# Graph convolution, two layers: a block's own-row transposes and products at the end of the preceding group of sums

## The chip, the cores and the metric

The kernel runs on one core of a Trainium2 chip. A core has TensorE (PE: matmuls and transposes, results in PSUM), VectorE (DVE), ScalarE (ACT), GpSimd (POOL) and SyncE (SP), each with its own queue, worked in order. GpSimd issues the gathers (indirect DMAs), SyncE the plain transfers. The metric is the device time of one execution in microseconds (us); lower is better.

## The reference

A graph has 6,250 nodes with 512 features each and 100,000 edges, sorted by their destination. The layer is two Chebyshev convolutions with a normalization between them, on normalized input, added to the input:

```python
norm = -dinv[src] * dinv[dst]                 # dinv = 1/sqrt(number of edges out of a node)
def prop(h):                                  # sum over the edges into each node
    return segment_sum(h[src] * norm[:, None], dst, num_segments=N)
def _cheb_conv(x, W0, W1, b):
    return x @ W0 + prop(x) @ W1 + b

h = relu(_layernorm(x))
h = _cheb_conv(h, W1_0, W1_1, b1)
h = layer_norm(h, gamma, beta)
h = where(h >= 0, h, 0.01 * h)
out = x + _cheb_conv(h, W2_0, W2_1, b2)
```

All is in float32. For each layer and each node, one row of 512 numbers has to be fetched per incoming edge and summed, and two products with 512 x 512 matrices have to be formed: that of the node's own row with W0, and that of the summed rows with W1.

## The kernel before

**Edges: chunks, units, groups.** The edges are cut into 782 chunks of 128 per layer. One gather fetches the 128 source rows of a chunk (2 KB each) into a slot of `places`, a ring of slots in SBUF. In layer 0 the first slots come from lent tiles too; from then on the ring has `R` = RE + NB - 2 KD = 14 + 49 - 8 = 55 slots, and it shrinks later. Three chunks make a unit, four units a group: a group has 12 chunks, and there are 66 groups per layer (group 0 has a single unit, so group g begins with chunk 3 x (4g - 3) for g > 0). `gather_to`, at the head of a group, issues all gathers whose slots were last used by groups before it; in GpSimd's queue each waits until the sums that used its slot are done.

**Sums.** For a group, VectorE forms selection matrices (`choose`, L650; in layer 0 also scaled by a column that the gather brought, `scale`, L690). `sums` runs 12 products of 128 x 32 by 128 x 512 (two matmuls each, L706), four units side by side into one PSUM tile `ps`. ScalarE copies it to `agg` (L721; in some early groups of layer 0 the tile is named `pre`).

**Blocks.** The nodes are cut into 49 blocks of 128. A block's summed rows lie in two or three neighbouring groups (`inside[i]`); it is due in the first group after these (`inside[i].stop`), so that three of four groups have one due block. For example block 2 is due in group 6, block 3 in group 7, block 4 in group 8, none in group 9, block 5 in group 10. The steps of a block are:

- `own`: four transposes of the block's own rows (tile `h`, loaded two blocks ahead by SyncE, or rows kept in SBUF) into the PSUM tile `hT_ps` (L596), and a copy by ScalarE to `hT` (L598, one buffer).
- `place`: two or three products of a 0/1 matrix `there` (VectorE, L729) with `agg`, into `an_ps` (L742). ScalarE scales the result to `an` (L841).
- `first_half`: four transposes of `an` into another `hT_ps` tile (L849; the name has two buffers), a copy by VectorE to `aT` (L851), and the products of `hT` with the layer's own-row matrix, eight matmuls (L608), into a new tile `u_ps` (two buffers), kept in `started[i]`.
- `second`: eight more matmuls of `aT` with the other matrix into the same `u_ps` (L608), and then `finish`: bias, normalization and leaky relu on VectorE and ScalarE (L810 to L824) and a store to the table of layer 1, or in layer 1 the result and its store to the output.

**Order.** The queues of TensorE, GpSimd and SyncE are in the order of the program; those of VectorE and ScalarE are put in order by the framework's planner. `turn` does `own`, then `second` of the blocks that wait for it (`left`), then `place` and the scaling, for a block that is due. In a group with a due block, TensorE's order is: `own` of it, `second` of the block before, `place`, the group's sums, `first_half` (transposes of `an`, own-row products). In groups 3 to 5 of layer 0 (`SOON`) the `turn` comes after the sums. From group 54 on (`NS - JOIN`), `second` follows `first_half` directly. The last four blocks (`EARLY`) have their own-row products formed separately. In layer 0 some further matmuls are spread over the groups: those that find the scale of the first 76 chunks (`look_up`, `find`, done by group 5), `end_matrices` after group 13, and from group 33 on the steps of `check`, which tests the assumptions on the edges.

Of the kernel before, what the change touches and what calls it, by code (L numbers as in the profile page):

```python
# [9 lines left out]
F32 = mybir.dt.float32  # L10
# [11 lines left out]
P = 128  # L22
# [13 lines left out]
JOIN = 12  # L36
# [415 lines left out]
def usual_path(tc, have):  # L452
# [8 lines left out]
    SOON = range(3, 6)  # L461
    EARLY = {NB - 4: NS - 13, NB - 3: NS - 11, NB - 2: NS - 9, NB - 1: NS - 7}
# [5 lines left out]
    inside = []  # L468
# [3 lines left out]
    with ExitStack() as es:  # L472
        pool = es.enter_context(tc.tile_pool(name="main", bufs=2))
        psum = es.enter_context(tc.tile_pool(name="main_ps", bufs=2, space=bass.MemoryType.PSUM))
# [3 lines left out]
        own_h, own_x, agg, placed, started, pre, late, theres = {}, {}, {}, {}, {}, {}, {}, {}  # L478
# [112 lines left out]
        def own(layer, i):  # L591

            h, r = own_h.pop(i), rows[i]
            ps = psum.tile([P, KD, P], F32, name="hT_ps")
            for kc in range(KD):
                nc.tensor.transpose(ps[:, kc, :r], h[:r, kc * P : (kc + 1) * P], ident[:r, :r])  # L596
            hT = pool.tile([P, KD, P], F32, name="hT", bufs=1)
            nc.scalar.activation(hT[:, :, :r], ps[:, :, :r], AF.Copy)  # L598
            return hT
# [6 lines left out]
        def products(u_ps, hT, w, r, start, stop, some=range(KD)):  # L606
            for kc in some:
                nc.tensor.matmul(u_ps[:r], hT[:, kc, :r], w[:, kc, :], start=(start and kc == 0),  # L608
                                 stop=(stop and kc == KD - 1))
# [113 lines left out]
        def spots(i, some):  # L723

            r = rows[i]
            there = [pool.tile([P, P], F32, name="there", bufs=3) for _ in some]
            for t, g in zip(there, some):
                m = Q * (unit[g + 1] - unit[g])
                behind[1] = nc.vector.tensor_scalar(t[:m, :r], iota_r[:m, :r], node_of[:m, g : g + 1],  # L729
                                                    -(1.0 + i * P), op0=OP.subtract, op1=OP.is_equal)  # L730
            return there
# [14 lines left out]
        def end_matrices():  # L746

            r = rows[END]
            at = pool.tile([P, D], F32, name="xt")[:, :r]
            nc.vector.tensor_scalar_add(at, iota_r[:, :r], 1.0 + END * P)  # L750
            ps = psum.tile([P, D], F32, name="u_ps")[:, :r]
            nc.tensor.matmul(ps, ones.to_broadcast([P, P]), own_row.pop(0)[:, :r], start=True, stop=True)
            for g, t in end_there.items():
                m = Q * (unit[g + 1] - unit[g])
                nc.vector.scalar_tensor_tensor(t[:m], at[:m], node_of[:m, g : g + 1], ps[:m], op0=OP.is_equal,
                                               op1=OP.mult)
# [72 lines left out]
        def turn(layer, i, left=()):  # L829

            r = rows[i]
            if layer == 1 and i not in EARLY:
                load_x(i)
            if i + AHEAD < NB:
                load(layer, i + AHEAD)
            hT = None if i in EARLY else own(layer, i)
            for k, aT in left:
                second(layer, k, aT)
            place(layer, i, [g for g in inside[i] if i < NB - 1 or g == NS - 1])
            an = pool.tile([P, D], F32, name="an")  # L840
            nc.scalar.activation(an[:r], placed.pop(i)[:r], AF.Copy,  # L841
                                 scale=(ndeg if layer == 1 and i not in EARLY else ndinv)[:r, i : i + 1])
            return hT, an

        def first_half(layer, i, hT, an, between=None):
            r = rows[i]
            ps = psum.tile([P, KD, P], F32, name="hT_ps")
            for kc in range(KD):
                nc.tensor.transpose(ps[:, kc, :r], an[:r, kc * P : (kc + 1) * P], ident[:r, :r])  # L849
            aT = pool.tile([P, KD, P], F32, name="aT", bufs=1)  # L850
            behind[2] = nc.vector.tensor_copy(aT[:, :, :r], ps[:, :, :r])  # L851
            if between is not None:
                between()
            if i not in EARLY:
                started[i] = psum.tile([P, D], F32, name="u_ps")
                products(started[i], hT, w_late[:, 1] if layer else w_sb[1], rows[i], True, False)
            return aT
# [11 lines left out]
        def dense(layer, i, hT, an, between=None):  # L869
            second(layer, i, first_half(layer, i, hT, an, between))  # L870

        def check():

            wrong = pool.tile([1, 8], F32, name="wrong", bufs=1)
            n = 0

            def count(v, op, than):
                nonlocal n
                w = v.shape[-1]
                ok = pool.tile([P, D], F32, name="xt")[0:1, :w]  # L880
                nc.vector.tensor_single_scalar(ok, v, than, op=op)
                nc.vector.tensor_reduce(wrong[:, n : n + 1], ok, AX.X, OP.add)
                n += 1

            for at, num in ((1, min(D, NC - 1)), (1 + D, NC - 1 - D)):
                if num > 0:
                    ps = psum.tile([P, D], F32, name="u_ps")[0:1, :num]
                    nc.tensor.matmul(ps, ident[:, 0:1], dlx[:, at + 1 : at + 1 + num], start=True, stop=False)
                    nc.tensor.matmul(ps, minus, dlx[:, at : at + num], start=False, stop=True)
                    count(ps, OP.is_lt, 0.0)  # L890
                    yield
            of = pool.tile([P, D], F32, name="xt")[0:1, :]
            nc.vector.tensor_sub(of[:, :NU], first[0:1, 1 : NU + 1], first[0:1, :NU])
            count(of[:, :NU], OP.is_gt, float(Q - 1))
            m = NS - 1
            of = pool.tile([P, D], F32, name="xt")[0:1, :]
            nc.vector.scalar_tensor_tensor(of[:, :m], iota_r[0:1, :m], -NQ * UN, first[0:1, unit[1] : NU : NQ],
                                           op0=OP.mult, op1=OP.add)
            nc.vector.tensor_scalar_add(of[:, :m], of[:, :m], -mean[1])
            nc.vector.tensor_mul(of[:, :m], of[:, :m], of[:, :m])  # L900
            count(of[:, :m], OP.is_gt, float(DRIFT * DRIFT))
            count(of[:, m - 1 : m], OP.is_gt, float(drift[m] * drift[m]))
            yield
            halves = [(lo, min(lo + D, NC)) for lo in range(0, NC, D)]
            assert len(halves) == 2
            for j, (lo, hi) in enumerate(halves):
                up = pool.tile([P, D], F32, name="xt")[:, : P - 1]
                nc.vector.tensor_sub(up, ident[:, 1:], ident[:, : P - 1])
                ps = psum.tile([P, D], F32, name="u_ps")[: P - 1, : hi - lo]
                nc.tensor.matmul(ps, up, dlx[:, 1 + lo : 1 + hi], start=True, stop=True)  # L910
                ok = pool.tile([P, D], F32, name="xt")[: P - 1, : hi - lo]
                nc.vector.tensor_single_scalar(ok, ps, 0.0, op=OP.is_lt)
                nc.vector.tensor_reduce(unsorted[: P - 1, j : j + 1], ok, AX.X, OP.add)
                yield
            ps = psum.tile([P, D], F32, name="u_ps")[0:1, 0:1]
            for j in range(2):
                nc.tensor.matmul(ps, unsorted[: P - 1, j : j + 1], ones[: P - 1, 0:1], start=(j == 0), stop=(j == 1))
            nc.vector.tensor_copy(wrong[:, n : n + 1], ps)
            n += 1
            ok = pool.tile([P, D], F32, name="xt")[0:1, 0:1]  # L920
            nc.vector.tensor_reduce(ok, wrong[:, :n], AX.X, OP.add)
            nc.vector.tensor_single_scalar(unseen, ok, 0.0, op=OP.is_gt)
# [9 lines left out]
        for layer in range(2):  # L932
# [4 lines left out]
            i, chosen, left = 0, {}, []  # L937
            for g in range(NS - 1):
# [9 lines left out]
                due = []  # L948
# [68 lines left out]
                    find("hT_ps")  # L1017
                if g < NS - JOIN - 1 and inside[i].stop <= g + 1:
                    theres[i] = spots(i, inside[i])
                for k, (hT, an) in due:  # L1020
                    if g < NS - JOIN:
                        left.append((k, first_half(layer, k, hT, an)))
                    else:
                        dense(layer, k, hT, an)
                if layer == 0:
                    look_up("hT_ps")
                    find("hT_ps")
                    if g >= NS // 2:
                        next(checking, None)
# [378 lines left out]
```

## Time and profile before

| | |
|---|---|
| time, median of three runs | 2024.12 us (2021.15 to 2028.18) |
| the profiled execution, its own time | 2021.31 us |
| span of its profile, first to last instruction | 2019.4 us |
| mean granted TensorE clock | 0.92 of full speed |
| instructions in the profile | 19,064 |
| gathers (L270, L515, L526) | 1,564 |
| moved by DMA | 510.33 MB, 253 GB/s in the mean |

All rows below come from the one profiled execution. A row of the timeline gives the start and the length in microseconds, the engine, the line of the kernel, the operation, the tiles written and read, their shapes and the count of merged instructions; in brackets stands the idle time of the engine ahead of it and what ended it. In rows of groups, the number after the busy time is the mean of one instruction in ns. Matmuls are pipelined, so that the start of the next one tells more than the length printed.

### The profile page before, as it was taken

The numbers are of one execution on the slowest core, as the hardware profiler recorded it, in microseconds if no ns is written. First come the engines' busy times: TensorE is split into PE (matmuls) and PEld (weight loads), VectorE is DVE, ScalarE is ACT, GpSimd is POOL, SyncE is SP. The second block draws the span as 40 slices with busy tenths as digits, with TensorE's granted clock in tenths as the row PEclk, the third lists the DMA queues.
The fourth block names the chain that finished last, engine by engine and source line by source line (L and its number), as shares of the span: only waits on it lengthen the run. The fifth ranks groups of instructions, "written<-read, shape, count | busy, mean of one in ns | idle before, by whom it ended". The sixth has DMA issues, their size and how long they took to land.

```text
span 2019.4 us, 19064 instructions
## 1 busy us (share of the span) xinstructions
PE 1665.2 (82%) x6850; PEld 663.2 (33%) x6850; DVE 681.6 (34%) x1454; ACT 389.0 (19%) x703; POOL 1489.1 (74%) x1578
## 2 busy tenths in 40 slices
PE   5589998677887776888888888888888888888898
PEld 4444443222333222333323322223322323333333
DVE  8975453323244233343352111122111211112221
ACT  7895221111111111111111011011010101011110
POOL 5477777777777777777777777777777777777774
PEclk9889999888998888999999999989999999989999
DMA  9998888887888887888877887787777778788875
GB/s 334 392 376 258 249 252 247 239 241 238 269 248 242 241 243 231 252 258 242 252 237 242 244 255 243 236 247 246 228 243 243 244 234 240 230 253 262 273 234 173
DMA packets 180278, 510.33 MB, mean 253 GB/s; under 512 B 33615, under 2 KB 35389, under 8 KB 180173
## 3 DMA queue, kind: packets, MB, share of 16 engines
q0 software_dynamic: 125120, 415.88, 68.5%
q1 hardware_dynamic: 55013, 93.12, 12.9%
q8 instruction: 56, 0.92, 0.2%
q14 instruction: 49, 0.40, 0.1%
q10 hardware_dynamic: 40, 0.02, 0.0%
HBM read 470.01 MB, written 38.86 MB: 252 GB/s over the span
## 4 chain that ended last, share of the span: by engine, by line
POOL 39%; PE 21%; DMA 17%; issue 16%; DVE 5%; ACT 2%; POOLq 0%; DVEq 0%; SPq 0%; ACTq 0%
POOL places L515 39%; DMA places<-tab,sidx 12%; PE u_ps L608 10%; PE ps L706 6%; PE an_ps L742 3%; DMA places<-tab,lidx 2%; ACT places L576 1%; DVE lo L382 1%; DVE hi L382 1%; PE hT_ps L849 1%; DMA dst_c<-in_dst_dram 1%; DMA places<-in_x_dram,sidx 1%; PE hT_ps L596 1%; DMA tab<-places 1%; DVE st L813 0%
## 5 line engine op out<-in xcount | busy, mean ns | idle before, releaser
L515 POOL DMA_INDIRECT places<-tab,sidx x1191 | 1130.1, 949 | 364.1 <-issue 327.5
L706 PE MATMUL ps<-places,sel 128*32 128x512 f32 x3104 | 511.0, 667 | 143.1 <-DMA places<-tab,sidx 86.6
L742 PE MATMUL an_ps<-agg,there 128*128 128x512 f32 (+1 forms) x554 | 268.6, 617 | 95.8 <-ACT agg L721 91.8
L515 POOL DMA_INDIRECT places<-tab,lidx x270 | 255.5, 946 | 82.3 <-issue 78.9
L706 PEld LDWEIGHTS ps<-places,sel 128*32 128x32 f32 x3104 | 102.0, 117 | 519.2 <-issue 194.6
L650 DVE TENSOR_TENSOR sel<-dlx,nodes_ps 128x384 f32<-128x384 f32 (+3 forms) x134 | 72.3, 541 | 417.5 <-PE ps L706 405.6
L608 PE MATMUL u_ps<-w,hT 128*128 128x512 f32 (+1 forms) x400 | 185.4, 607 | 20.7 <-ACT hT L598 20.2
L721 ACT ACTIVATE agg<-ps 128x512 f32<-128x512 f32 (+2 forms) x130 | 76.2, 588 | 610.0 <-PE ps L706 583.5
L608 PE MATMUL u_ps<-places,hT 128*128 128x512 f32 (+2 forms) x408 | 185.4, 598 | 2.9 <-ACT hT L598 2.9
L742 PEld LDWEIGHTS an_ps<-agg,there 128*128 128x128 f32 (+1 forms) x554 | 104.9, 197 | 216.8 <-issue 108.3
L608 PE MATMUL u_ps<-w,aT 128*128 128x512 f32 x384 | 173.1, 593 | 3.1 <-DVE aT L851 3.1
L608 PE MATMUL u_ps<-places,aT 128*128 128x512 f32 x384 | 173.4, 593 | 0.8 <-DVE aT L851 0.8
L690 DVE TENSOR_TENSOR sel<-sel,places 128x384 f32<-128x384 f32 (+9 forms) x76 | 35.1, 468 | 331.9 <-DMA places<-tab,sidx 331.9
L804 DVE SCALAR_TENSOR_TENSOR u_ps<-u_ps,root,bias 128x512 f32<-128x512 f32 x45 | 34.1, 758 | 284.8 <-PE u_ps L608 284.8
L598 ACT ACTIVATE hT<-hT_ps 128x512 f32<-128x512 f32 (+1 forms) x98 | 58.2, 594 | 291.3 <-PE hT_ps L596 290.9
L608 PEld LDWEIGHTS u_ps<-w,hT 128*128 128x128 f32 (+1 forms) x400 | 73.7, 194 | 96.7 <-issue 74.8
L608 PEld LDWEIGHTS u_ps<-places,hT 128*128 128x128 f32 (+1 forms) x408 | 75.7, 196 | 78.5 <-issue 73.6
L816 ACT ACTIVATE sd<-mv,eps 128x1 f32<-128x1 f32 (+1 forms) x49 | 14.4, 294 | 441.1 <-DVE mv L814 441.1
L270 POOL DMA_INDIRECT places<-in_x_dram,sidx x63 | 59.6, 947 | 52.6 <-ACT junk L286 19.0
L729 DVE TENSOR_SCALAR there<-iota_r,node_of 128x128 f32<-128x128 f32 (+1 forms) x286 | 68.2, 307 | 89.4 <-PE an_ps L742 89.4
L608 PEld LDWEIGHTS u_ps<-w,aT 128*128 128x128 f32 x384 | 70.7, 190 | 83.2 <-issue 78.6
L608 PEld LDWEIGHTS u_ps<-places,aT 128*128 128x128 f32 x384 | 70.6, 190 | 80.3 <-issue 78.3
(200 smaller groups left out, 1245.3 us busy)
## 6 DMA issues: line engine op xcount, KB each, us to landing
places<-tab,sidx POOLq DMA_INDIRECT x1191, 3.8
h<-tab SPq DMA_DIRECT2D x70, 256.0 KB
xt<-in_x_dram SPq DMA_DIRECT2D x48, 256.0 KB
out_dram<-t SPq DMA_DIRECT2D x48, 256.0 KB
tab<-places SPq DMA_DIRECT2D x22, 528.0 KB
places<-in_x_dram SPq DMA_DIRECT2D x5, 1792.0 KB
tab<-t SPq DMA_DIRECT2D x26, 256.0 KB
tab<-places SPq DMA_DIRECT2D x20, 256.0 KB
```

Source lines behind the costliest of these rows:

```text
L270: nc.gpsimd.indirect_dma_start(out=lent[t] if t < X else places[:, t - X, :D], out_offset=None, in_=x, in_offset=bass.IndirectOffsetOnAxis ...
L382: nc.vector.tensor_tensor(t, s[:, g * 2 * GJ : (g + 1) * 2 * GJ].rearrange("p (j s) -> p j s", s=2)[:, :, None, :] .to_broadcast([EP, GJ, ...
L515: nc.gpsimd.indirect_dma_start(out=places[:, slot(t), :] if own_scale else zr(layer, t), out_offset=None, in_=x if layer == 0 and t < RAW ...
L598: nc.scalar.activation(hT[:, :, :r], ps[:, :, :r], AF.Copy)
L608: nc.tensor.matmul(u_ps[:r], hT[:, kc, :r], w[:, kc, :], start=(start and kc == 0), stop=(stop and kc == KD - 1))
L650: nc.vector.tensor_tensor(sel[:, q : q + k, :w, :], of, node[:, q : q + k, None, :].to_broadcast([P, k, w, Q]), op=OP.is_equal)
L690: last = nc.vector.tensor_tensor(v, v, places[:, k : k + hi - lo, D : D + 1].to_broadcast([P, hi - lo, Q]), op=OP.mult)
L706: members.append(nc.tensor.matmul(to, sel[:, q, s, :], rows_of, start=(s == 0), stop=(s == len(chunk[q]) - 1 and (cnt is None or chunk[q][ ...
L721: nc.scalar.activation(agg[g][: n * Q, lo : lo + w], ps[: n * Q, lo : lo + w], AF.Copy)
L729: behind[1] = nc.vector.tensor_scalar(t[:m, :r], iota_r[:m, :r], node_of[:m, g : g + 1], -(1.0 + i * P), op0=OP.subtract, op1=OP.is_equal)
L742: all_of.append(nc.tensor.matmul(placed[i][:r], t[:m, :r], agg[g][:m, :], start=(g == inside[i][0]), stop=(g == inside[i][-1])))
L804: nc.vector.scalar_tensor_tensor(v, v, root[:r, i : i + 1], bias2[:r], op0=OP.mult, op1=OP.add)
```

## The change

At the end of a group, after the sums, the kernel looks at the next block. If it is due in the next group (`inside[i].stop <= g + 1`), fewer than two blocks are due in this one, the group is before group 52 (`NS - JOIN - 2`), and it is layer 1 or group 6 or later, then `own` of that block is issued there, ahead of `first_half` of the block due in this group, and the products of `hT` follow it, into a `u_ps` tile that is kept in `started`. `turn` and `first_half` leave both out for a block that is in `started`. Four helper tiles in PSUM, in `end_matrices` and `check`, take buffers of the name `hT_ps` instead of `u_ps`.

```diff
 def end_matrices():
-            ps = psum.tile([P, D], F32, name="u_ps")[:, :r]
+            ps = psum.tile([P, D], F32, name="hT_ps")[:, :r]
...
 def turn(layer, i, left=()):
-            hT = None if i in EARLY else own(layer, i)
+            hT = None if i in EARLY or i in started else own(layer, i)
...
 def first_half(layer, i, hT, an, between=None):
-            if i not in EARLY:
+            if i not in EARLY and i not in started:
                 started[i] = psum.tile([P, D], F32, name="u_ps")
                 products(started[i], hT, w_late[:, 1] if layer else w_sb[1], rows[i], True, False)
...
 def check():                                   # in three places
-                    ps = psum.tile([P, D], F32, name="u_ps")[0:1, :num]
+                    ps = psum.tile([P, D], F32, name="hT_ps")[0:1, :num]
...
 # the loop over the groups, after the sums of group g
                 if g < NS - JOIN - 1 and inside[i].stop <= g + 1:
                     theres[i] = spots(i, inside[i])
+                ahead_of = (g < NS - JOIN - 2 and inside[i].stop <= g + 1 and len(due) < 2
+                            and (layer == 1 or g >= SOON.stop))
+                if ahead_of:
+                    next_hT = own(layer, i)
                 for k, (hT, an) in due:
                     if g < NS - JOIN:
                         left.append((k, first_half(layer, k, hT, an)))
                     else:
                         dense(layer, k, hT, an)
+                if ahead_of:
+                    started[i] = psum.tile([P, D], F32, name="u_ps")
+                    products(started[i], next_hT, w_late[:, 1] if layer else w_sb[1], rows[i], True, False)
```

More of the change, by code (lines that the diff above doesn't have):

```diff
@@ L908, in check @@
                 nc.vector.tensor_sub(up, ident[:, 1:], ident[:, : P - 1])
-                ps = psum.tile([P, D], F32, name="u_ps")[: P - 1, : hi - lo]
+                ps = psum.tile([P, D], F32, name="hT_ps")[: P - 1, : hi - lo]
                 nc.tensor.matmul(ps, up, dlx[:, 1 + lo : 1 + hi], start=True, stop=True)
@@ L914, in check @@
                 yield
-            ps = psum.tile([P, D], F32, name="u_ps")[0:1, 0:1]
+            ps = psum.tile([P, D], F32, name="hT_ps")[0:1, 0:1]
             for j in range(2):
```

## The prediction

> **What bounds the kernel now.** I read the page first: its span, its busy times, and its chain that ended last.
>
> ```profile
> span 2019.4 us, 19064 instructions
> ## 1 busy us (share of the span) xinstructions
> PE 1665.2 (82%) x6850; PEld 663.2 (33%) x6850; DVE 681.6 (34%) x1454; ACT 389.0 (19%) x703; POOL 1489.1 (74%) x1578
> ...
> POOL 39%; PE 21%; DMA 17%; issue 16%; DVE 5%; ACT 2%; POOLq 0%; DVEq 0%; SPq 0%; ACTq 0%
> ```
>
> TensorE is busier than GpSimd (82% against 74%), yet the chain runs through GpSimd. So the next view is GpSimd's groups of instructions from 129 us to the last gather. Columns: busy time and mean of one, then the idle time just before them and what ended it.
>
> ```profile
> L515 POOL DMA_INDIRECT places<-tab,sidx x1191 | 1130.1, 949 | 364.1 <-issue 327.5 <-DMA places<-tab,sidx 19.8 <-ACT places L576 3.9
> L515 POOL DMA_INDIRECT places<-tab,lidx x270 | 255.5, 946 | 82.3 <-issue 78.9 <-DMA places<-tab,lidx 2.7 <-PE ps L706 0.6
> L526 POOL DMA_INDIRECT places<-tab,eidx x27 | 27.7, 1026 | 8.2 <-issue 7.9 <-DMA tab<-pre 0.3
> ```
>
> The idle time is 364.1 / 1191 = 0.306 us and 82.3 / 270 = 0.305 us per gather, nearly all put down to issue. A gather therefore takes 0.95 us and 0.30 us of pause, 1.25 us, and GpSimd never rests otherwise. These 1,488 gathers at 1.25 us are 1860.0 us; busy and idle times add up to 1867.9. Only 7.9 us in the whole stretch are anything but the bare pace. The timeline of GpSimd gives its ends:
>
> ```profile
> 129.13 0.94 POOL L270 DMA_INDIRECT places<-in_x_dram,sidx  x1 [0.65 <-ACT pre L721]
> ...
> 2000.90 0.94 POOL L515 DMA_INDIRECT places<-tab,lidx  x1 [0.30 <-issue]
> ```
>
> After the last gather, 2019.4 - 2001.8 = 17.6 us are left for its landing, the last sums and the last two blocks. None of that is touched: the change stops at group 51 of 66 in each layer. So the time moves only if GpSimd is made to wait, or is spared a wait. The table by stretches says where that can be. Columns: length of the stretch, busy time of PE, PEld, DVE, ACT and POOL, granted clock, DMA share, GB/s.
>
> ```profile
> 200.00:300.00 100.00, 100.00 (x448) 40.87 (x444) 49.43 (x113) 22.07 (x39) 75.02 (x79) 1.00 0.83 250
> 300.00:650.00 350.00, 272.89 (x1111) 106.81 (x1104) 126.35 (x291) 51.58 (x93) 264.82 (x280) 0.89 0.82 246
> ...
> 1060.00:1500.00 440.00, 373.07 (x1428) 131.60 (x1420) 88.53 (x196) 46.09 (x74) 333.06 (x352) 0.93 0.79 243
> ```
>
> Between 200 and 300 us TensorE is never idle: it has more work ready than it gets done. Later it idles 22% (272.89 of 350) and 15% (373.07 of 440). The place to look at is thus early in layer 0, where TensorE is late and a gather may have to wait for its slot.
>
> **The pinch.** GpSimd's timeline there:
>
> ```profile
> 200.90 1.02 POOL L515 DMA_INDIRECT places<-tab,sidx  x1 [0.30 <-issue]
> 203.33 0.94 POOL L515 DMA_INDIRECT places<-tab,sidx  x1 [1.41 <-ACT pre L721]
> ```
>
> Counted from 0 in GpSimd's order, the gather at 203.33 is number 130. The ring has 14 + 49 - 8 = 55 slots here, so it reuses that of chunk 75, the first of group 7 (3 x 25). It waits for all sums of group 7. TensorE's rows from the end of group 6's sums to the end of group 7's:
>
> ```profile
> 189.23 0.66 PE L849 MATMUL hT_ps<-ident,an 128*128 128x128 f32 x4
> 189.72 3.60 PE L608 MATMUL u_ps<-w,hT 128*128 128x512 f32 x8
> 193.16 0.60 PE L596 MATMUL hT_ps<-ident,h 128*128 128x128 f32 x4
> 193.59 3.60 PE L608 MATMUL u_ps<-w,aT 128*128 128x512 f32 x8
> 197.03 1.02 PE L742 MATMUL an_ps<-agg,there 128*128 128x512 f32 x2
> 197.89 1.02 PE L742 MATMUL an_ps<-pre,there 128*128 128x512 f32 x2
> 198.74 1.02 PE L742 MATMUL an_ps<-agg,there 128*128 128x512 f32 x2
> 199.70 2.78 PE L706 MATMUL ps<-places,sel 128*32 128x512 f32 x24
> 202.41 0.66 PE L849 MATMUL hT_ps<-ident,an 128*128 128x128 f32 x4
> ```
>
> From start to start: transposes of the aggregate 0.49 us, own-row products 3.44, own-row transposes 0.43, second half of a block 3.44, placing 2.67, sums 2.71. The sums of group 7 end at 202.41 and the gather starts 0.92 us later. There is no slack at all: it had already waited 1.41 us instead of 0.30. ScalarE's copies in the same stretch:
>
> ```profile
> 189.33 0.60 ACT L721 ACTIVATE agg<-ps 128x512 f32<-128x512 f32 x1 [0.74 <-PE ps L706]
> 193.85 0.60 ACT L598 ACTIVATE hT<-hT_ps 128x512 f32<-128x512 f32 x1 [3.92 <-PE hT_ps L596]
> ```
>
> A copy of 0.60 us follows the sums by 0.10 us (189.23 to 189.33), and the hT copy follows the end of its transposes by 0.09 us (193.76 to 193.85).
>
> **The change part by part.** Nothing is added or removed. For 35 blocks of layer 0 (3 to 37) and 38 of layer 1 (0 to 37), four transposes, one ScalarE copy and eight matmuls (0.43, 0.60 and 3.44 us) come before the next group instead of within it. No DMA and no GpSimd instruction is among them. SyncE's load of a later h tile waits for the same transposes and comes free no later. Two u_ps tiles are now alive at once, all that there are; the next one needs VectorE to have finished the block before, with placing and sums (2.67 + 2.71 us) between: a wait here would stand where the hT wait stands, and I take 0 for it. Giving u_ps tiles to hT_ps in the end matrices and the checks changes no instruction; what it costs is at most a wait for a buffer in groups with spare TensorE time, taken as 0.
>
> *Group 6, paid once.* Block 2 has not been started early, since the condition begins with this group. So group 6 ends with the products of block 2 and those of block 3: one run of 3.44 us moves ahead of the sums of group 7. In steady state each group loses a run and gains one; here it only gains. There is also a wait: hT has one buffer, so block 3's copy can start only when block 2's products have read it. The aggregate's transposes now start at 189.66, block 2's products at 190.15; they end 3.60 us later, at 193.75. Copy from 193.84 to 194.44, and 0.05 us to TensorE (the row at 806.24 below follows its copy's end at 806.19 by that). TensorE was free at 193.59, so it stands 0.90 us. Together 0.90 + 3.44 = 4.34 us before the sums of group 7, which end at 206.75. Gather 130 starts at 207.67.
>
> *Each later block.* Where a block was also due, TensorE issues own transposes and aggregate transposes (0.43 + 0.49 = 0.92 us), and the products wait for ScalarE's two copies: 0.10 + 0.60 + 0.60 + 0.05 = 1.35 us. New stall: 0.43 us. Where no block was due, the cover is 0.43 us and the stall 0.92. Where no own rows follow, the products no longer cover the aT copy. The trace has that case at the end of layer 1:
>
> ```profile
> 1979.87 3.70 PE L608 MATMUL u_ps<-places,aT 128*128 128x512 f32 x8 [0.78 <-DVE aT L851]
> ```
>
> 0.78 us. In a cycle of four groups (three blocks) that makes 0.92 + 0.43 + 0.43 + 0.78 = 2.56 us on TensorE, in 48 gathers or 60 us. In the later stretches 15% to 22% of 60 us, 9 to 13 us, are idle and hide it; the bounds are 0 and 2.56 us a cycle, and I take 0. If that cover were gone, the 24 such cycles (11 and 13) would cost 61 us.
>
> *The next gather that could wait.* After gather 130 this is number 142, freed by group 8:
>
> ```profile
> 212.88 2.78 PE L706 MATMUL ps<-places,sel 128*32 128x512 f32 x24
> 215.59 0.66 PE L849 MATMUL hT_ps<-ident,an 128*128 128x128 f32 x4
> ```
>
> ```profile
> 218.56 0.95 POOL L515 DMA_INDIRECT places<-tab,sidx  x1 [0.30 <-issue]
> ```
>
> Its sums move by 4.34 + 0.43 = 4.77 us, to end at 220.36, and free it at 221.28. GpSimd, itself 4.34 us late, comes to it at 222.90. It does not wait, with 1.62 us to spare. Group 9 then gives a run of products back (block 4's ran a group earlier), so the lead grows.
>
> *The sum.* GpSimd loses 4.34 us once and keeps its pace after it. The profiled execution took 2021.3 us, 1.9 above its span: 2021.3 + 4.34 = 2025.7 us, 0.21% slower. The median of the runs, 2024.1, lies 2.8 us above that execution; counted from it the same step gives 2028.5. Bounds of the step: 0, if the copies fall so that nothing is late, and 7.4 us with the colder clock below. About 0.3%, 6.1 us, is what a measurement of this kernel can tell from no change, so the forecast counts as no change.
>
> **The clock.** Does a short stall make TensorE slow? After 2.44 us of waiting, the 24 matmuls of a group took 4.32 us instead of the 2.78 above:
>
> ```profile
> 423.46 4.32 PE L706 MATMUL ps<-places,sel 128*32 128x512 f32 x24 [2.44 <-DVE sel L690]
> ```
>
> After 0.78 us, the eight matmuls at 1979.87 took 3.70 instead of 3.60. The new stalls are 0.43 to 0.92 us, so I charge nothing. A rule speaks against this: the Trainium skill (TensorE: Matmul & The Clock Gate, "A second HAM failure mode: psum-queue depth-cycling") says that frequent micro-idles between groups of matmuls can make the clock gate swing to half rate and back. The trace bears it out for 2.44 us, not for 0.78. By that rule the first rival below is the case.
>
> **The rivals.** *Colder clock, a little slower.* Each new stall at the ends of groups 6 and 7 brings one slow start of 4.32 - 2.78 = 1.54 us. The sums of group 7 come 4.34 + 1.54 = 5.88 us late, those of group 8 4.77 + 3.08 = 7.85. Gather 142 is freed at 224.36 and reached at 224.44: it just doesn't wait, and the time is 2021.3 + 5.9 = 2027.2 us; with a third slow start among them, now unspared, 2028.7. For it: the granted clock of 0.89 from 300 us on. Against it: the row after 0.78 us. It decides from stalls of some 1 to 2 us on.
>
> *ScalarE holds hT, slower than before.* In layer 0, ScalarE runs its queue in order, and the statistics of a block (sd) wait for VectorE, which waits for gathers:
>
> ```profile
> 805.41 0.29 ACT L816 ACTIVATE sd<-mv,eps 128x1 f32<-128x1 f32 x1 [30.26 <-DVE mv L814]
> 805.61 0.58 ACT L721 ACTIVATE agg<-ps 128x512 f32<-128x512 f32 x1
> 806.09 0.59 ACT L598 ACTIVATE hT<-hT_ps 128x512 f32<-128x512 f32 x1
> ```
>
> ```profile
> 806.24 2.08 PE L742 MATMUL an_ps<-agg,there 128*128 128x512 f32 x2 [17.66 <-ACT agg L721]
> ```
>
> ```profile
> 812.49 0.95 POOL L515 DMA_INDIRECT places<-tab,sidx  x1 [0.30 <-issue]
> ```
>
> Placing waited 17.66 us for agg; now the products wait as long for hT, and placing comes after them. The hT copy comes 0.48 us after that of agg, and the products take 3.44, so the sums after such a group come 3.9 us later. The gather at 812.49 reuses a slot of group 49, whose copy began at 805.61: 6.9 us of slack. From a delay of more than that, gathers wait, and two such groups past it cost about 2 x 3.9 us: 2025.7 + 7.8 = 2033.5. Against it: one such delay is smaller than the slack, and group 49's own sums lose a run of products.
>
> *No effect.* The planner's order of ScalarE or VectorE offsets the early stall: 2021.3. For it: only 1.1 us of the wait at 203.33 stand against the pace. Against it: TensorE is full there, and 3.44 us are put ahead of what gather 130 needs.
>
> *Faster.* Products would cover TensorE's waits for agg. Against it: GpSimd does not feel those. All that it could regain is 7.9 us, so 2013.4 at the very best, and gaining 6.1 would need three quarters of it.
>
> **How the numbers follow.** Forecast 0.54, colder clock or longer stalls 0.18, ScalarE's queue 0.13, no effect 0.11, faster 0.04. Within 0.3% fall no effect, half of the colder clock (2027.2 is just inside 6.1 us) and 0.42 of the forecast: 0.62. Slower are ScalarE's queue, the other half of the colder clock and the 0.12 of the forecast that I leave to runs scattered upward: 0.34. The likeliest is 2025.7 us. The range reaches from 2020.0 (no effect, in a run like the lowest shown, 2021.2, and 1 us of spread) to 2034.0 (ScalarE's case, or the colder clock's 2028.7 with the 2.8 us of the median and some spread).
>
> **What would show it.** Right: the gather after the twelve that group 6 freed waits about 5 to 6 us (1.41 before), the sums of group 7 end near 206.8, gather 142 does not wait, and the gathers after it keep 1.25 us to the end, with the last one near 2005.2 and the same 17.6 us behind it. New stalls of 0.4 to 0.9 us stand ahead of the own-row products, put down to ACT hT, and 0.8 us ahead of the second half of every third block. Wrong: waits of GpSimd above 0.3 us after 230 us; a wait at gather 130 of 1.41 us or less; another tail after the last gather; or the 24 matmuls of groups 7 to 12 at over 4 us.

## The result and the profile after

The changed kernel takes 2028.1 us in the median of 20 runs (2026.1 to 2032.9), the one before 2024.3 in 20 runs (2021.0 to 2028.2). The ratio is 1.0023, with a 95% interval of 1.0017 to 1.0029: slower by 3.9 us between the medians, within the 0.3% that was set as no change, and clear of zero. The forecast was 4.3 us more than before (2025.7 counted from the profiled execution, 2028.5 from the median).

The profiled execution of the changed kernel lies in the upper part of its runs: 2030.9 us, a span of 2029.1. Its page, busy times and the chain that ended last:

```profile
span 2029.1 us, 19114 instructions
...
PE 1663.1 (82%) x6850; PEld 670.1 (33%) x6850; DVE 687.3 (34%) x1454; ACT 388.6 (19%) x703; POOL 1491.3 (73%) x1578
...
POOL 35%; PE 27%; DMA 15%; issue 14%; DVE 6%; ACT 3%; SPq 0%; POOLq 0%; DVEq 0%; ACTq 0%
```

The counts of TensorE's, VectorE's, ScalarE's and GpSimd's instructions are those of before. GpSimd's groups from 129 us to the last gather (busy time and mean of one, then the idle time before):

```profile
L515 POOL DMA_INDIRECT places<-tab,sidx x1191 | 1131.8, 950 | 372.8 <-issue 326.6 <-DMA places<-tab,sidx 22.2 <-ACT pre L721 9.5
L515 POOL DMA_INDIRECT places<-tab,lidx x270 | 255.6, 947 | 82.3 <-issue 77.1 <-DMA places<-tab,lidx 4.3 <-PE ps L706 0.6
```

The idle time of the first group has grown from 364.1 to 372.8 us, and its third releaser is new: 9.5 us put down to the aggregate's copy of group 7, which starts when that group's sums end. One gather holds nearly all of it. It is number 130, and the last gather follows:

```profile
211.31 0.94 POOL L515 DMA_INDIRECT places<-tab,sidx  x1 [9.23 <-ACT pre L721]
...
2010.81 0.95 POOL L515 DMA_INDIRECT places<-tab,lidx  x1 [0.31 <-issue]
```

Before, that gather started at 203.33 after 1.41 us. The rows of TensorE between the sums of group 6 and those of group 7 tell why:

```profile
192.76 0.66 PE L596 MATMUL hT_ps<-ident,h 128*128 128x128 f32 x4
193.25 0.60 PE L849 MATMUL hT_ps<-ident,an 128*128 128x128 f32 x4
193.69 3.60 PE L608 MATMUL u_ps<-w,hT 128*128 128x512 f32 x8
198.03 3.70 PE L608 MATMUL u_ps<-w,hT 128*128 128x512 f32 x8 [0.75 <-ACT hT L598]
201.57 3.60 PE L608 MATMUL u_ps<-w,aT 128*128 128x512 f32 x8
205.01 1.02 PE L742 MATMUL an_ps<-agg,there 128*128 128x512 f32 x2
205.86 1.02 PE L742 MATMUL an_ps<-pre,there 128*128 128x512 f32 x2
206.72 1.02 PE L742 MATMUL an_ps<-agg,there 128*128 128x512 f32 x2
207.67 2.78 PE L706 MATMUL ps<-places,sel 128*32 128x512 f32 x24
210.39 0.66 PE L596 MATMUL hT_ps<-ident,h 128*128 128x128 f32 x4
```

There are two runs of own-row products now (193.69 and 198.03), with a wait of 0.75 us between by the bracket, or 0.90 us counted from start to start (198.03 - 193.69 - 3.44). The copy that the second run waits for starts 0.09 us after the first run has ended (193.69 + 3.60 = 197.29):

```profile
197.38 0.60 ACT L598 ACTIVATE hT<-hT_ps 128x512 f32<-128x512 f32 x1 [3.92 <-PE u_ps L608]
```

What ended ScalarE's wait is the run of products that reads the one hT buffer. From the end of one group's sums to the end of the next pass 210.39 - 192.76 = 17.63 us; before it was 202.41 - 189.23 = 13.18. That is 4.45 us more, where 4.34 were forecast: the wait is 0.90 us of it, the second run 3.54 (201.57 - 198.03). Gather 130 starts 0.92 us after the sums, as before.

The two profiled spans differ by 9.7 us, though, and not by 4.4. They split up so: 3.53 us because the sums of group 6 ended later (192.76 against 189.23), in a stretch where TensorE's and ScalarE's instructions and their order are the same in both kernels; 4.45 us between groups 6 and 7; 1.93 us between gather 130 and the last one (1799.50 against 1797.57 us), as more of the gathers took over 0.1 us above the pace (22 against 15) and the others a trifle longer, with no new wait; and -0.2 us behind the last gather (17.3 against 17.6). The first part varies from run to run: in six kernels below that are the same up to there (one block alone, without the early groups, the three with repeated products, without the first block), they end anywhere between 190.1 and 195.7 us.

### The profile page after: what moved, and what is told of

Read it like the earlier page. It is cut to its first block, busy times and chain, and to the rows that moved or that the text cites. A ratio compares the mean times of both kernels' runs of the same rounds, so it can differ in the third digit from the quotient of the medians.

```text
span 2029.1 us, 19114 instructions
## 1 busy us (share of the span) xinstructions
PE 1663.1 (82%) x6850; PEld 670.1 (33%) x6850; DVE 687.3 (34%) x1454; ACT 388.6 (19%) x703; POOL 1491.3 (73%) x1578
## 4 chain that ended last, share of the span: by engine, by line
POOL 35%; PE 27%; DMA 15%; issue 14%; DVE 6%; ACT 3%; SPq 0%; POOLq 0%; DVEq 0%; ACTq 0%
POOL places L515 35%; PE u_ps L608 14%; DMA places<-tab,sidx 10%; PE ps L706 6%; PE an_ps L742 4%; DMA places<-tab,lidx 3%; DVE hi L382 1%; ACT hT L598 1%; DVE lo L382 1%; DMA w<-in_L_gnn_W_dram 1%; ACT agg L721 1%; DVE st L813 1%; DVE u_ps L810 1%; DMA places<-in_x_dram,sidx 0%; ACT places L576 0%
## 5 line engine op out<-in xcount | busy, mean ns | idle before, releaser
L515 POOL DMA_INDIRECT places<-tab,sidx x1191 | 1131.8, 950 | 372.8 <-issue 326.6
L706 PE MATMUL ps<-places,sel 128*32 128x512 f32 x3104 | 478.7, 642 | 106.6 <-DMA places<-tab,sidx 68.5
L608 PE MATMUL u_ps<-w,hT 128*128 128x512 f32 (+1 forms) x400 | 209.9, 673 | 140.5 <-ACT hT L598 137.0
L742 PE MATMUL an_ps<-agg,there 128*128 128x512 f32 (+1 forms) x554 | 255.6, 595 | 5.2 <-DVE rs L819 5.2
L608 PEld LDWEIGHTS u_ps<-w,hT 128*128 128x128 f32 (+1 forms) x400 | 81.6, 215 | 238.3 <-ACT hT L598 146.9
L841 ACT ACTIVATE an<-an_ps,ndeg 128x512 f32<-128x512 f32 x45 | 31.0, 688 | 342.0 <-PE an_ps L742 342.0
```

Of the source, the lines that this page charges most:

```text
L515: nc.gpsimd.indirect_dma_start(out=places[:, slot(t), :] if own_scale else zr(layer, t), out_offset=None, in_=x if layer == 0 and t < RAW ...
L706: members.append(nc.tensor.matmul(to, sel[:, q, s, :], rows_of, start=(s == 0), stop=(s == len(chunk[q]) - 1 and (cnt is None or chunk[q][ ...
L742: all_of.append(nc.tensor.matmul(placed[i][:r], t[:m, :r], agg[g][:m, :], start=(g == inside[i][0]), stop=(g == inside[i][-1])))
L841: nc.scalar.activation(an[:r], placed.pop(i)[:r], AF.Copy, scale=(ndeg if layer == 1 and i not in EARLY else ndinv)[:r, i : i + 1])
```

## The experiments

The theory: GpSimd paces the kernel, and the change makes it wait once, at gather 130, for a run of products that now stands ahead of the sums of group 7. The main rival: the 73 moved blocks each add short stalls to TensorE, and these add up. A second one was that TensorE's work is on the path throughout. Ratios are to the kernel before on the same chip, with 95% intervals.

**One block alone.**

```diff
-                            and (layer == 1 or g >= SOON.stop))
+                            and layer == 0 and g == SOON.stop)
```

> The change for one block only: block 3 of layer 0, at the end of group 6. The other 72 blocks stay as before. Theory (GpSimd waits once, at gather 130, for the sums of group 7): the whole cost is here, +4.3 us against before, the ratio 1.002, the same as the full change; gather 130 waits some 4.3 us longer. Rival (the short stalls of the 73 blocks add up): one block of 73, so +0.1 us, ratio 1.000.

Measured: 2029.2 us against 2024.9, ratio 1.0022 (1.0013 to 1.0032). One moved block of 73 costs as much as all. In its trace, TensorE goes from the end of group 6's sums to that of group 7's in 207.75 - 190.12 = 17.63 us, as in the full change:

```profile
190.12 0.66 PE L596 MATMUL hT_ps<-ident,h 128*128 128x128 f32 x4
...
195.40 3.70 PE L608 MATMUL u_ps<-w,hT 128*128 128x512 f32 x8 [0.75 <-ACT hT L598]
...
205.04 2.78 PE L706 MATMUL ps<-places,sel 128*32 128x512 f32 x24
207.75 0.66 PE L849 MATMUL hT_ps<-ident,an 128*128 128x128 f32 x4
```

Its gather 130 waited 4.25 us, which is 2.8 us longer than before and not the 4.3 that were expected, because GpSimd itself came to it later in this execution (204.4 us against 201.9). Set beside the full change, a start 2.6 us earlier (190.12 against 192.76) is most of the difference to 9.23; the rest is where GpSimd stood (it had waited longer earlier).

**All blocks but the early ones.**

```diff
-                            and (layer == 1 or g >= SOON.stop))
+                            and (layer == 1 or g >= 13))
```

> The change without the early groups: layer 0 only from group 13 on, layer 1 as in the change; 30 and 38 of the 73 blocks. Theory of the pinch: gathers of the slots used from group 13 on have over 7 us of slack, so 0 us against before, ratio 1.000 within 0.001, and no wait of GpSimd above 0.3 us after gather 130. Rival of the stalls that add up: 68 of 73 blocks, so +3.6 us, ratio 1.0018.

Measured: 2025.0 us against 2024.9, ratio 1.0004 (0.9993 to 1.0015). 68 blocks cost nothing that can be seen; the 1.0018 of the stalls lies outside the interval. The four helper tiles that take buffers of another name are in this kernel too, so nothing can be seen of them either. GpSimd's groups carry 368.0 us of idle time in the first one (364.1 before), 3.9 us of it at gather 130, where this execution's late start shows (sums of group 6 to 194.06, then 13.19 us, as before).

**The same work twice, without the change, at the pinch and behind it.** In the kernel before, in `first_half`:

```diff
                 started[i] = psum.tile([P, D], F32, name="u_ps")
+                if layer == 0 and i == 2:                 # or: i in range(8, 36, 3)
+                    products(started[i], hT, w_sb[1], rows[i], True, True)
                 products(started[i], hT, w_late[:, 1] if layer else w_sb[1], rows[i], True, False)
```

> The kernel before, with the own-row products of block 2 (layer 0, end of group 6) computed twice: eight matmuls, 3.44 us more on TensorE ahead of the sums of group 7, and nothing moved. Theory of the pinch: +3.4 us against before, ratio 1.0017, though TensorE idles for some 350 us in the whole. Rival (TensorE has room, the cost of the change is in its new waits): 0 us.

Measured: 2028.6 us against 2024.9, but the ratio of 1.0010 has an interval of 0.9999 to 1.0022, which holds the theory's 1.0017 and, just, 1.0000. By the times this is open. The trace shows 212.27 - 195.66 = 16.61 us between the sums, 3.43 more than before, and 8.31 us of wait at gather 130.

> The kernel before, with the own-row products of ten blocks of layer 0 (8, 11, 14 to 35, due in groups 14, 18, 22 to 50) computed twice: 80 matmuls, 34 us more on TensorE, all behind the pinch. Theory: TensorE's idle time in those groups takes them, 0 us against before, ratio 1.000 within 0.001. Rival (TensorE's work is on the path all along): +34 us, ratio 1.017.

Measured: 2024.0 us against 2024.9, ratio 0.9998 (0.9989 to 1.0007). Ten extra runs of products, 34 us of TensorE, cost nothing behind the pinch.

To close what the single extra run left open, the same with four extra runs (`for _ in range(4)` for block 2):

> The kernel before, with the own-row products of block 2 at the end of group 6 computed five times: 32 more matmuls, 13.8 us of TensorE ahead of the sums of group 7, all of it work that the result does not need. Theory of the pinch: nearly all of it arrives at the end, +13 to +14 us, ratio 1.0065, and gather 130 waits about 14 us longer than in the kernel before. Rival (TensorE's later idle time takes it): 0.

Measured: 2038.9 us against 2024.7, ratio 1.0078 (1.0064 to 1.0091), 13 to 18 us. The three rows that carry it, two of TensorE and one of GpSimd:

```profile
191.35 17.33 PE L608 MATMUL u_ps<-w,hT 128*128 128x512 f32 x40
...
215.06 2.78 PE L706 MATMUL ps<-places,sel 128*32 128x512 f32 x24
```

```profile
218.70 0.94 POOL L515 DMA_INDIRECT places<-tab,sidx  x1 [15.20 <-ACT pre L721]
```

The work reaches the end in full: the last gather starts 2015.05 - 218.70 = 1796.4 us after gather 130. In the other kernels of these two sets that have no further wait it is 1796.4 to 1796.9 us, in the one before 1797.6. Behind the last gather pass 17.2 to 17.9 us in all of these. The start of gather 130 thus settles the time, to some 1.5 us.

**Without the first block.**

```diff
-                            and (layer == 1 or g >= SOON.stop))
+                            and (layer == 1 or g >= 7))
```

> The change without its first block: layer 0 from group 7 on, layer 1 as in the change; 72 of 73 blocks. Now the sums of group 8 are the first to get a run of products more ahead of them (4.3 us with the hT wait), and gather 142 has 2.1 us of slack. Theory of the pinch: +2.3 us, ratio 1.0011, the wait at gather 142 and not at 130. Rival of the stalls: as the full change, +4, ratio 1.002.

Measured: 2027.2 us against 2024.7, ratio 1.0017 (1.0008 to 1.0026). Both sizes lie in the interval, so the time doesn't tell the two apart; the place does. The wait appears where the theory puts it, at gather 142:

```profile
225.33 0.94 POOL L515 DMA_INDIRECT places<-tab,sidx  x1 [2.48 <-PE ps L706]
```

It is 2.18 us above the usual 0.30, where 2.3 were expected. This gather follows the end of the sums that it waits for by 0.45 us (224.88 to 225.33), where gather 130 follows ScalarE's copy, 0.92 us after the sums. (Gather 130 waited too, 5.22 us, behind a late start: the sums of group 6 ended at 194.07.) The late start moves both gathers alike, so the slack of some 2 us at the second one stays.

**Relieving the pinch.** If the theory holds, sums that come earlier should gain. Groups 3 to 5 already do their sums first.

```diff
-    SOON = range(3, 6)
+    SOON = range(3, 9)
```

> The kernel before, with groups 6 to 8 of layer 0 also of the kind that does its sums first and the due block after them (as groups 3 to 5 do). The own transposes (0.43), second half (3.44) and placing (2.67) of a block move from ahead of the sums of group 7 to behind them: these come some 6 us earlier. Theory of the pinch: the wait at gather 130 is gone; faster by what it cost, 1 to 5 us as the start of a run falls, ratio 0.998. Rival (the time is set elsewhere): 0.

The same range stands in L717, so that the edit also gives the aggregate of group 9 a tile of the name `pre` instead of `agg`.

Measured: 2026.1 us against 2024.7, ratio 1.0007 (0.9998 to 1.0017). It is not faster: this expectation failed. TensorE's rows show a wait that has grown and a new one:

```profile
176.86 2.78 PE L706 MATMUL ps<-places,sel 128*32 128x512 f32 x24
...
189.75 5.33 PE L706 MATMUL ps<-places,sel 128*32 128x512 f32 x18 [4.62 <-ACT places L576]
195.01 0.86 PE L596 MATMUL hT_ps<-ident,h 128*128 128x128 f32 x4
195.71 1.02 PE L742 MATMUL an_ps<-pre,there 128*128 128x512 f32 x2
196.57 1.02 PE L742 MATMUL an_ps<-agg,there 128*128 128x512 f32 x2
197.43 1.02 PE L742 MATMUL an_ps<-pre,there 128*128 128x512 f32 x2
199.23 0.66 PE L849 MATMUL hT_ps<-ident,an 128*128 128x128 f32 x4 [0.78 <-ACT an L841]
...
203.25 2.78 PE L706 MATMUL ps<-places,sel 128*32 128x512 f32 x24
205.96 0.66 PE L596 MATMUL hT_ps<-ident,h 128*128 128x128 f32 x4
```

The sums of group 6 cannot come earlier, because they need rows that ScalarE still has to scale (L576); they wait 4.62 us instead of 1.84 and run slower after it (5.33 us for 18 matmuls instead of 2.76). What stood ahead of them had been cover. Then the transposes of `an` follow its scaling with nothing between, 0.78 us a block. The sums of group 7 come 2.2 us nearer to those of group 6 (10.95 us against 13.18), but that only makes up for the later sums of group 6: from the start of group 5's sums, up to which TensorE's order is the same in both kernels, to the end of group 7's pass 205.96 - 176.86 = 29.10 us, and before it was 202.41 - 173.41 = 29.00. Nothing was gained ahead of gather 130. It waited 3.77 us in this execution, and gather 154 waited 1.47. This execution also took 2.8 us longer behind the last gather (20.4 us against 17.6), at the end of layer 1, where the edit changes nothing. So the start of the pinch is set by ScalarE as well as by TensorE, which my theory had left out.

> The changed kernel with the same three groups doing their sums first; by its own condition the change then begins at group 9 of layer 0. 33 and 38 blocks keep the change. Theory of the pinch: the cost of the change is gone, the same time as the kernel before with these groups, ratio 0.998 against before. Rival of the stalls: 71 blocks still cost 4 us more than that.

Measured: 2027.6 us against 2024.7, ratio 1.0018 (1.0008 to 1.0028). The expected 0.998 failed here too. The interval overlaps with that of 1.0007, and 1.0018 is also what the rival could give; the difference of the two, 1.5 us, is not clear of noise. In its trace GpSimd has waits at the same two gathers as without the change (1.90 and 1.47 us, there 3.77 and 1.47) and none behind them, which speaks for the theory, but the times settle nothing.

**The wait for the hT buffer, and a second try at relief.** Two more kernels, an own tile for block 3's `hT`, and only groups 7 and 8 with their sums first:

```diff
+            if layer == 0 and i == 3:
+                hT = pool.tile([P, D], F32, name="xt").rearrange("p (k e) -> p k e", k=KD)
+            else:
                 hT = pool.tile([P, KD, P], F32, name="hT", bufs=1)
```

```diff
-                soon = layer == 0 and g in SOON
+                soon = layer == 0 and (g in SOON or g in (7, 8))
```

> The changed kernel with the own rows of block 3 of layer 0 copied to a tile of their own instead of the one hT buffer, so that the copy need not wait for block 2's products. One look at the trace: the wait of TensorE ahead of block 3's products (0.75 us in the changed kernel) is gone, and from the end of the sums of group 6 to the end of those of group 7 pass 16.8 to 16.9 us, against 17.6 in the changed kernel and 13.2 in the one before. The rest of the 4.4 us, the run of products itself (3.4), stays. Rival (the wait is for ScalarE's queue, not for the buffer): 17.6 as before.

> The kernel before, with groups 7 and 8 of layer 0 doing their sums first, and group 6 left as it was (so that its sums do not stand longer for ScalarE's scaling, the 4.6 us seen with groups 6 to 8). The sums of group 7 come right after block 2's products, 6.5 us earlier in TensorE's order. Theory of the pinch: no wait above 0.3 us at gather 130, and what it cost is gained, 1 to 4 us, ratio 0.9985. Rival (as with groups 6 to 8, the new wait of the aggregate's transposes for ScalarE, 0.78 us a block, and the next gathers take it back): 0 or +1 us.

> The same kernel as own3_apart, which fell on a chip where the kernel before takes 2,381 us and GpSimd waits at many places, so that it cannot be set beside the other runs. Expected as there: no wait ahead of block 3's products, 16.8 to 16.9 us from the end of the sums of group 6 to those of group 7 (17.6 in the changed kernel, 13.2 before); in time 0.7 us less than the changed kernel, ratio to before 1.0018, more than these runs can tell. Rival (ScalarE's queue holds the copy): 17.6.

> The same kernel as soon78, for the same reason. Theory of the pinch: no wait above 0.3 us at gather 130, 1 to 4 us gained, ratio 0.9985. Rival (the aggregate's transposes wait 0.78 us a block for ScalarE, and a later gather takes the gain back): ratio 1.000.

All four runs fell on another chip, where the kernel before takes 2381 us and the granted clock is 0.85 to 0.87. GpSimd there waits in many places, mostly 12 gathers after the wait before, and more often than not for what the trace only calls `remote`:

```profile
POOL places L515 <- issue: 396.9, 1290, 4.0
POOL places L515 <- remote: 156.4, 63, 4.3
```

(the waits of GpSimd with the own tile: total, count, longest). On that chip GpSimd is not simply at its pace, so these runs cannot test the pinch. Groups 7 and 8 first gave ratios of 0.9999 (0.9975 to 1.0024) and 0.9988 (0.9968 to 1.0009); both intervals hold 1 as well as the expected 0.9985, so they decide nothing. Gather 130 waited 1.71 us in one of their traces and 0.30 in the other, and gather 142 then 2.60 and 3.36. The changed kernel with the own tile took 18.0 us in both traces from the end of group 6's sums to that of group 7's (245.74 to 263.73 and 240.08 to 258.09), where 16.8 to 16.9 were expected: this expectation failed. Ahead of block 3's products stood a wait of 0.21 us in the single run and of 1.13 in the other, as ScalarE came to its copies late there (its copy of the aggregate began 4.5 us after the sums in both, at 250.24 and 244.60, where it is 0.10 in the kernel before on the ordinary chip). Whether the wait for the buffer can be had back on the ordinary chips stays open. The kernel with the own tile took 2373.4 us against 2381.8 in the second set, ratio 0.9963 (0.9942 to 0.9985), and 2376.4 in the single run. It contains the full change, so there the change, with that tile, gains rather than loses. Which of the two does it, and through what, was not tried.

## Why the prediction was right or wrong, point by point

**What bounds the kernel.** Right, and shown. GpSimd's pace carries the time: 34 us of extra TensorE work behind the pinch cost nothing, 13.8 us ahead of gather 130 cost 13 to 18.

**The step at group 6.** Right in place and size: 4.45 us instead of 4.34. The wait for the one hT buffer is the 0.90 us of the prediction, counted as there from start to start, and the second run of products took 3.54 us instead of 3.44, a slower start that had been charged at nothing. One block alone gives the whole cost. The measured 3.9 us (4.7 by the ratio, whose interval is 3.4 to 5.9) are this step. That gather 130 has no slack is true of the profile from which it was read. In that of the ten repeated products, with the same order up to there, it did not wait: its slot was free at 204.42 + 0.92 = 205.34 us, and GpSimd came to it at 205.76. In such an execution the step would cost 0.4 us less, by this estimate. The single figure of 2025.7 us lies 2.4 below the measured median, as it was counted from a profiled execution 3.0 us below the median of the kernel before; counted from the median, 2028.5, it is met to 0.4.

**The later stalls.** Right that GpSimd does not feel them; from group 13 on they cost nothing. Their sizes, from start to start as the prediction counts: with a block due, 0.47 us instead of 0.43 (0.31 in the brackets); with no block due, 0.9 to 1.0 us instead of 0.92 (0.75 in the brackets, once 1.05) in the early groups, and far longer later, below. With aT uncovered it is the 0.78 us that had been taken from a bracket. No wait is put down to a u_ps buffer, as assumed. TensorE's waits in the changed kernel (total, count, longest):

```profile
PE u_ps L608 <- ACT hT L598: 157.3, 80, 17.6
PE ps L706 <- DMA places<-tab,sidx: 68.5, 43, 6.1
...
PE u_ps L608 <- DVE aT L851: 22.4, 27, 1.6
```

The waits for `agg` ahead of placing, 91.8 us before, are gone from this list, and the waits for gathers fell from 86.6 to 68.5 us. In their place stand 157.3 us ahead of the own-row products (23.2 before). The waits changed their place more than their sum.

**Gather 142.** Right that it does not wait with the full change (0.31 us); without block 3 moved it waited 2.48. Its slot comes free 0.45 us after the sums, not 0.92 as was taken over from gather 130, so that the prediction made the slack 0.5 us too small.

**The colder clock.** This rival did not occur. After waits of 0.31 and 0.75 us the eight matmuls took 3.70 us, and the 24 of groups 7 and 8 still 2.78; the granted clock from 200 to 300 us stayed at 1.00:

```profile
200.00:300.00 100.00, 95.40 (x401) 38.51 (x403) 44.79 (x99) 18.52 (x34) 69.14 (x73) 1.00 0.76 228
```

The Trainium skill's warning about micro-idles (TensorE: Matmul & The Clock Gate, "A second HAM failure mode: psum-queue depth-cycling") is not borne out for pauses of this length. Long ones do show slow starts, as the next row.

**ScalarE holds hT.** The mechanism is there, the cost is not. Where placing had waited 17.66 us, the products now wait as long and then run slowly (5.75 us for eight matmuls instead of 3.60):

```profile
816.00 5.75 PE L608 MATMUL u_ps<-w,hT 128*128 128x512 f32 x8 [17.65 <-ACT hT L598]
```

No gather waited for it: the step from the gather before does not exceed 1.7 us anywhere between there and the end of the layer. The slack of 6.9 us held, as the argument against this rival had it.

**What would show it.** Three numbers came out otherwise: gather 130 waited 9.23 us, not 5 to 6, the sums of group 7 ended at 210.4, not 206.8, and the last gather started at 2010.8, not near 2005.2. The first two are the start of that execution, 3.5 us later, which the prediction took as fixed; the third adds the 1.9 us between gather 130 and the last one. The start is a part of the spread: where gather 130 waits, each microsecond by which the sums of group 6 end later is one by which it starts later, in both kernels.

**No effect, and faster.** Neither occurred. The bound on a gain, 7.9 us of GpSimd time above its pace, was not tested by this change.

## What to carry to other kernels

Where one queue issues without pause, work on the other engines costs nothing until an instruction of that queue has to wait for it, so look for the few places where its waits exceed its pace, and ask of each moved step whether it lands ahead of what they need. A step that is moved forward by one period, ahead of something for which that queue waits, costs its whole length once, at the first period, and nothing after; putting the start behind the pinch takes the cost away (here the change from group 13 on), while leaving out only the first period moves a part of it to the next one (here from gather 130 to gather 142, ratio 1.0017). And before you bring work forward to relieve a pinch, see what the stretch that it passes was covering: here it was ScalarE's scaling.

## What the runs showed of the hardware that was not expected

- The beginning of the kernel varies by up to 6.4 us from run to run with the same instructions of TensorE and ScalarE in the same order (in eight kernels the sums of group 6 end between 189.2 and 195.7 us), while from gather 130 to the last one pass 1796.4 to 1799.5 us in all kernels that have no wait on the way, on the ordinary chips.
- One chip ran the kernel before in 2381 us instead of 2024, at a granted clock of 0.85 to 0.87 instead of 0.92. There is no trace of that kernel there. In the changed one with the own tile, GpSimd waited up to 4.3 us at 63 gathers for what the profile only calls "remote", ScalarE's copy of group 6's aggregate began 4.5 us after the sums instead of 0.10, and the mean traffic was 215 GB/s instead of 253.
- A gather follows the end of the sums that free its slot by 0.45 us at gathers 142 and 154, and by 0.92 us at gather 130, where the trace names ScalarE's copy as the last release.
